# Reordering GpSimd's scatters, two statistics and two rank requests at the end of layer 0's attention

## The chip, the cores and the metric

The kernel runs on one core of a Trainium2 chip, as one launch. The metric is device time in microseconds (us); lower is better. The time before is the median of three runs. The profile comes from one further execution of the same kernel, taken with the hardware profiler. Engine names are those of the profile: PE (TensorE, matrix products), DVE (VectorE), ACT (ScalarE), POOL (GpSimd), SP (SyncE, which here only issues DMAs).

## What is computed

The reference is two pre-norm transformer layers on x of shape (8, 1024, 128). This case lies in layer 0 alone, at the end of its attention and the start of its expert feed-forward:

```python
x = x + attention(layernorm(x))        # layer 0: 8 heads of 32, softmax over 1024 keys
n = layernorm(x)
logits = n @ gate_w.T                  # 14 experts
top2_p, top2_i = top_k(softmax(logits), 2)
w = top2_p / max(sum(top2_p), 1e-10)
x = x + (n + w0 * expert(top2_i[0], n) + w1 * expert(top2_i[1], n))
...                                    # layer 1: linear attention, then top-1 experts
```

`expert` is gelu(n @ w1 + b1) @ w2 + b2 with the weights of the chosen expert.

## The kernel before, in words

**Stage one, attention and routing.** For each of 8 batches the kernel makes softmax attention over 1024 tokens, eight heads as two groups of four. A *block* is a batch, a group and a half of the queries (512): 32 blocks in all. Each block takes 16 *steps* (8 key chunks `kc`, two steps `hp` each), so there are 512 steps, numbered h = 0 to 511. A list `todo[h]` holds pieces of other work (the projections and routing of a batch that is done, the normalisation of a batch to come), put there by `at(h, f)`; the loop runs them at the end of step h. On PE, DVE and ACT the program order of the trace is the order of the queue. On POOL it is not: the tile framework's scheduler orders POOL, and the kernel holds single instructions back with `keep_in_program_order` (used through `pinned`), which adds an edge to the instruction traced just before on the same engine. Such an edge orders the issue only; it is no semaphore wait.

**The steps around the change.** From step 488 on the loop is "quiet": no more block's maxima are made, and the DVE takes over the sums of exponentials (L777) that POOL made until then. In a quiet pair of steps, PE makes four heads' scores, ACT makes their exponentials (L383), PE weighs values (`num`, L397) and, every other pair, sums columns for the denominators (`den`, L397). Steps 496 to 511 are those of the last block. Order of issue, before, in the steps that matter (chunk pairs of step h and h+1 share one tile of exponentials):

| step | of the attention | pieces from `todo` |
|---|---|---|
| 490 | scores, num | `rank` of batch 6: PE `rk` (L567, L570), DVE picks (L576) |
| 491 | den; DVE sums L777 | `places` of batch 6: DVE L585 to L590, writes the row numbers `at` |
| 492, 493 | scores, num | shares of batch 6 (L527 to L537) |
| 494 | scores, num | `project` of the first half of batch 7: PE `op` (L448), DVE adds x (L453); `norm` |
| 495 | den; DVE sums L777 | `stats` (L266, L268), `power` (DVE `ve` L273, POOL `rs`) of that half |
| 496 | scores, num | `offset` (DVE `off`, L278), `scaled` (ACT `xn`, L291) |
| 497 | num; ACT copies the finished num to `nums` (L425) | `scaled` (ACT `xn`) |
| 498 | scores, first num of the last block | `turned`: PE `tp` (L299), ACT `xT` (L301) |
| 499 | den; ACT copies den to `dens` (L410); DVE sums L777 | `logits` of the half (L471 to L477) |
| 499 to 502 | eight quotients: DVE reciprocal L415, POOL product | `first` to `third` |
| 504, 505 | scores, num | `count` (DVE L545 to L561), `rank` |
| 506, 507 | scores, num; den; DVE sums L777 | `places`, `softmax` |

PSUM has one bank for `num` and one for `den` (pool `pvd`), three for `st` (pool `sc`) and three for `big` (pool `big`, which also serves `rk`, `op`, `tp` and `lg`).

**Scatters.** `places` appends 16 closures per batch (two experts times eight chunks; eight for each half of batch 7) to `moving`. The loop pops one per step when quiet, before it runs `todo`. Each closure, `move` (L594), is an indirect DMA issued by POOL that writes 128 rows of `xn` into `rows_in` at the rows in `at`. All scatters stand in a group `rows_in` whose members are declared free of dependencies on each other (L599, L600), and then are kept in program order (L601). Batch 6's 16 scatters are traced at steps 494 to 509. Batch 7's first half has two at steps 510 and 511 and six after the loop; its second half's eight follow those.

**After the loop** the second half of batch 7 goes through one chain: reciprocals and quotients (DVE, L807, L808), `project`, `stats`, `power`, `offset`, `scaled`, `turned`, `choice`, then all scatters left.

**Stage two, experts.** Tiles of 256 rows are read back from `rows_in` by SP (L916); the first weights are copied by DVE (L924) behind the last scatter.

**GpSimd's line.** The power (`ALU.pow`), the quotients and the sums run under the helper's line, L209; they are told apart by their tiles (`rs`, `outT`, `e`).

Of the kernel before, what the change touches and what calls it, by code (L numbers as in the profile page):

```python
# [12 lines left out]
ALU = mybir.AluOpType  # L13
# [4 lines left out]
NB = 8  # L18
# [60 lines left out]
def tile_two_layers(  # L79
# [5 lines left out]
    nc = tc.nc  # L85
# [22 lines left out]
    mhalf = keep.tile([P, CPB], F32, name="mhalf")  # L108
# [6 lines left out]
    rstds = [keep.tile([P, CPB], F32, name=f"rs{b}", tag=f"rs{b}") for b in range(NB)]  # L115
# [45 lines left out]
    def looked_up(table, nt, engine, top):  # L161
# [12 lines left out]

        return value


    layer0 = ctx.enter_context(ExitStack())
    routes = layer0.enter_context(tc.tile_pool(name="routes", bufs=1))
# [10 lines left out]
    nc.gpsimd.memset(counts, 0.0)  # L190
    found = routes.tile([P, NB, 2, CPB], U32, name="found")
    last_move = []
    layer0w = ctx.enter_context(ExitStack())
    blob = layer0w.enter_context(tc.tile_pool(name="blob", bufs=1)).tile([P, E0, B_END], F32, name="blob")

    with ExitStack() as ph:
# [11 lines left out]
        def pinned(f, *args, **kw):  # L208
            return tc.keep_in_program_order(f(*args, **kw))  # L209
# [46 lines left out]
        class Norm:  # L256
# [13 lines left out]
            def power(self):  # L270
                cs = slice(self.c0, self.c0 + self.n)
                ve = stat0.tile([P, self.n], F32, name=f"ve{self.n}")
                nc.vector.tensor_scalar(ve, mvs[self.b][:, cs, 1], LN_EPS, None, ALU.add)  # L273
                pinned(nc.gpsimd.tensor_tensor, rstds[self.b][:, cs], ve, mhalf[:, :self.n], ALU.pow)

            def offset(self):
                cs = slice(self.c0, self.c0 + self.n)
# [125 lines left out]
        def settle(n, qb, pieces):  # L403

            b, g = divmod(n, 2)
            if (b, 0) not in outs:
                outs[b, 0] = work.tile([P, 2, T], F32, name="outT", bufs=1)
            out_b, top = outs[b, 0], tops.pop(0)
            s = work.tile([P, BLK], F32, name="dens", bufs=1)
            nc.scalar.copy(s, vds.pop((n, qb, True)))  # L410
            w = BLK // pieces

            def divide(i):
                cols = slice(i * w, (i + 1) * w)
                nc.vector.reciprocal(s[:, cols], s[:, cols])  # L415
                pinned(
                    nc.gpsimd.tensor_tensor,
                    out_b[:, g, qb * BLK + i * w:qb * BLK + (i + 1) * w], top[:, cols], s[:, cols], ALU.mult,
                )

            return [lambda i=i: divide(i) for i in range(pieces)]

# [11 lines left out]
        class Finish:  # L434
# [144 lines left out]
            def places(self):  # L579

                n, b, c0 = self.n, self.b, self.c0
                ats = [stat0.tile([P, CPB], U32, name=f"at{k}") for k in range(2)]
                for k in range(2):
                    mine = ranks[:, k, b, c0:c0 + n]
                    nc.vector.tensor_reduce(mine, self.picks[k], AX.X, ALU.add)  # L585
                    to = self.tile("to", [P, n])
                    nc.vector.scalar_tensor_tensor(
                        to, chosen[:, k, b, c0:c0 + n], float(UNIT * REG0), mine, ALU.mult, ALU.add
                    )
                    nc.vector.tensor_scalar(ats[k][:, :n], to, float(TW0), None, ALU.add)  # L590
                xn = self.xn

                def move(j, k):
                    ins = nc.gpsimd.indirect_dma_start(  # L594
                        out=rows_in, out_offset=bass.IndirectOffsetOnAxis(ap=ats[k][:, j:j + 1], axis=0),
                        in_=xn[:, c0 + j, :], in_offset=None,
                    )

                    tc.declare_no_dep(ins.ins, group="rows_in", reason="rows are distinct")  # L599
                    tc.add_to_no_dep_group("rows_in", ins.ins)  # L600
                    tc.keep_in_program_order(ins)  # L601
                    last_move[:] = [ins.ins.name]

                moving.extend(lambda j=j, k=k: move(j, k) for k in range(2) for j in range(n))
# [39 lines left out]
        norm = Norm(1, 0, CPB, xn, xT[1])  # L644
# [30 lines left out]
        def at(h, f, *args):  # L675
            todo[h].append(lambda: f(*args))

        def normalised(h0, norm, stats, power, offset, scaled, turned):
            for i, h in enumerate(stats):
                at(h0 + h, lambda i=i: norm[0].stats(2 * i))  # L680
            at(h0 + power, lambda: norm[0].power())
            at(h0 + offset, lambda: norm[0].offset())
            for i, h in enumerate(scaled):
                at(h0 + h, lambda i=i: norm[0].scaled(2 * i))
            for i, h in enumerate(turned):
                at(h0 + h, lambda i=i: norm[0].turned(CPK * i))
# [24 lines left out]
        def complete(b):  # L711

            h0, f, norm = 64 * (b + 1), Finish(b, 0, CPB), []
            at(h0 + 8, f.project, 0)
            at(h0 + 17, f.project, CPK)
            at(h0 + 10, lambda: norm.append(f.norm()))
            normalised(h0, norm, (12, 14, 20, 22), 22, 26, (27, 28, 29, 30), (29, 32))
            hs = (36, 38, 37, 42, 46, 50, 47, 54, 56, 58, 62, 66)
            if b == NB - 2:
                hs = (33, 34, 34, 38, 39, 40, 40, 41, 42, 43, 44, 45)  # L720
            for h, piece in zip(hs, f.choice()):
                at(h0 + h, piece)

        def last_half():

            h0, f, norm = 64 * (NB - 1), Finish(NB - 1, 0, CPK), []
            at(h0 + 46, f.project, 0)
            at(h0 + 46, lambda: norm.append(f.norm()))
            normalised(h0, norm, (47, 47), 47, 48, (48, 49), (50,))
            for h, piece in zip((51, 52, 53, 53, 54, 55, 55, 56, 57, 58, 59, 60), f.choice()):  # L730
                at(h0 + h, piece)

        for b in range(NB):
            if b:
                complete(b - 1)
            if b + 1 < NB:
                prepare(b + 1)
        last_half()


        weighing, summing, dividing = None, None, []
        h = 0
        for n, qb in blocks:
            for kc in range(CPB):
                for hp in range(2):
# [9 lines left out]
                    if kc % 2 == 0:  # L755
                        if weighing is not None:
                            weigh(*weighing, den=False, half=hp)
                            if hp == 1 and weighing[2] == CPB - 1:
                                numerator(*weighing[:2])
                    elif hp == 0:  # L760
                        weigh(*weighing, den=False)
                    elif summing is not None and h < STEPS - 1:
                        weigh(*summing, den=True)
                        if summing[2] == CPB - 1:
                            dividing = settle(*summing[:2], pieces=8)
                            dividing.pop(0)()
# [33 lines left out]
        f = Finish(NB - 1, CPK, CPK)  # L800
        norm = f.norm()
# [43 lines left out]
    nil1 = wts1.tile([P, TI0, RW1], F32, name="nil1")  # L845
    counts1 = keep.tile([P, E1], F32, name="counts1")
    rows1 = dram.tile([ROWS1, RW1], F32, name="rows1")

    def behind(ins, name, kind=mybir.DependencyClass.NoSync):
        tc.add_manual_dep(  # L850
            ins, name, mybir.DependencyInfo(kind, mybir.DependencyReason.DATA), reason="the order of issue"
        )

    def load_layer1():
        nc.sync.dma_start(out=wq1_sb, in_=wq1)
# [41 lines left out]
    def tiles0(ph, first, last):  # L897
# [23 lines left out]
        def stage(j):  # L921
            e = expert_of(j)
            t = work.tile([P, 1, B_END], F32, name="wt", bufs=4)
            ins = nc.vector.tensor_copy(t, blob[:, bass.ds(e, 1), :]).ins  # L924
            if j == 0:

                behind(ins, last_move[0], mybir.DependencyClass.Sync)
            return t[:, 0, :]
# [114 lines left out]
    with ExitStack() as ph:  # L1043
# [22 lines left out]
        def stats(p):  # L1066

            x1 = tokens_of(p)
            st = stat1.tile([P, PAIR, 6], F32, name="bnst1")
            mv = stat1.tile([P, PAIR, 2], F32, name="mv1", bufs=6)  # L1070
            for i in range(PAIR):
                nc.vector.bn_stats(st[:, i, :], x1[:, i, :])
                nc.vector.bn_aggr(mv[:, i, :], st[:, i, :])
            ve = stat1.tile([P, PAIR], F32, name="ve1")
            nc.vector.tensor_scalar(ve, mv[:, :, 1], LN_EPS, None, ALU.add)
            rs = stat1.tile([P, PAIR], F32, name="rs1", bufs=6)
            ins = tc.keep_in_program_order(nc.gpsimd.tensor_tensor(rs, ve, mhalf[:, :PAIR], ALU.pow)).ins
            if gathered[0] == PAIR * NPAIR:
                for name in since:
                    behind(ins, name)  # L1080
            since.clear()
            norms[p] = mv, rs
# [22 lines left out]
        def behind_within(ins):  # L1105

            if products:
                behind(ins, products.pop(), mybir.DependencyClass.Sync)
# [782 lines left out]
```

## Time and profile before

| what | value |
|---|---|
| median of three runs (lowest, highest) | 2073.74 us (2072.45, 2079.61) |
| the profiled execution, its own time | 2022.9 us |
| span in its profile, first to last instruction | 2021.0 us |
| mean granted TensorE clock | 0.959 of full speed |
| busy share PE, DVE, ACT, POOL | 95%, 68%, 55%, 59% |
| scatters L594, all | 128, mean 1018 ns |
| scatters L594, issue to landing (median, 1215 to 1320 us) | 2.3 us |

The profile's page gives busy time by engine, the busy share in 40 slices of the span, and the costliest groups of instructions. Three further views are used below. The timeline of an engine lists its instructions in order of time: start, duration, engine, line and operation, written tile <- read tiles, count; in brackets the idle time of the engine just before, and what ended it. The table of windows gives for each stretch of time the busy time of each engine, and the granted TensorE clock as a fraction of full speed. The view of waits sums who waited for whom. All times count from the span's start. Attention fills the span up to about 1280 us; the experts' first matrix products follow at 1313 us.

### The profile page before, as it was taken

The page shows a single profiled execution, that of the slowest core. Times are in us where ns is not written, and L with a number is a line of the kernel's source. Part 1 is how long each engine was busy: PE and PEld are TensorE (multiplying, and loading weights), DVE is VectorE, ACT ScalarE, POOL GpSimd, SP SyncE. Part 2 cuts the span into 40 slices and gives each one's busy share as a digit, 9 for nine tenths or more (in the row PEclk, how much of TensorE's full clock was granted, in tenths as well). Part 3 has the DMA queues.
Part 4 walks back from the last instruction along what each step waited for, and adds up shares of the span by engine and source line. Part 5 has one row for each costly group of instructions (what it writes and reads, how often), then busy time and mean ns, then how long its engine had stood idle before and what let it go on. Part 6 is the DMA issues. An engine that isn't in the chain of part 4 may idle for free. (4 is left out here: it accounts for less than half of the span.)

```text
span 2021.0 us, 45115 instructions
## 1 busy us (share of the span) xinstructions
PE 1918.9 (95%) x17340; PEld 991.8 (49%) x17340; DVE 1379.7 (68%) x3551; ACT 1108.8 (55%) x2338; POOL 1201.7 (59%) x1312
## 2 busy tenths in 40 slices
PE   7999999999999999999999998499869999996997
PEld 3333333333333333333333333299847777775996
DVE  6677767768768768768767876566647777774453
ACT  3555565565565565565565455266546666662443
POOL 1466656667667667766766766433265576644455
PEclk9999999999999999999999998699969999996999
DMA  7000000000000000000000000044322221111332
GB/s 243 2 2 2 1 2 3 8 8 10 8 8 9 9 8 8 9 8 9 8 8 8 13 9 23 31 131 133 117 76 74 83 62 49 49 39 64 106 103 59
DMA packets 49407, 80.93 MB, mean 40 GB/s; under 512 B 13225, under 2 KB 32112, under 8 KB 49056
## 3 DMA queue, kind: packets, MB, share of 16 engines
q0 software_dynamic: 17552, 41.03, 6.2%
q1 hardware_dynamic: 28240, 28.97, 5.0%
q10 hardware_dynamic: 3392, 7.95, 1.3%
q8 instruction: 140, 2.29, 0.5%
q14 instruction: 83, 0.68, 0.1%
HBM read 42.08 MB, written 35.96 MB: 39 GB/s over the span
## 5 line engine op out<-in xcount | busy, mean ns | idle before, releaser
L344 DVE TENSOR_REDUCE nmp<-big 128x1 f32<-128x512 f32 x1000 | 642.1, 683 | 279.4 <-PE st L380 237.4
L383 ACT ACTIVATE e<-st 128x512 f32<-128x512 f32 x1000 | 544.1, 595 | 477.4 <-PE st L380 413.4
L209 POOL TENSOR_TENSOR e<-e 128x512 f32<-128x512 f32 x488 | 604.0, 1268 | 53.4 <-PE num L397 53.3
L340 PE MATMUL big<-kT,qT 32*128 32x512 f32 x2000 | 625.8, 640 | 0.7 <-DVE nmp L344 0.5
L380 PE MATMUL st<-qT,kT 32*128 32x512 f32 x2000 | 531.1, 588 | 0.0
L397 PE MATMUL num<-e,v 128*32 128x512 f32 x3064 | 301.4, 466 | 8.5 <-ACT nums L425 8.5
L209 POOL TENSOR_TENSOR outT<-nums,dens 128x64 f32<-128x64 f32 x248 | 80.7, 326 | 347.2 <-DVE dens L415 259.6
L380 PEld LDWEIGHTS st<-qT,kT 32*128 32x128 f32 x2000 | 213.9, 191 | 3.7 <-issue 1.7
L379 PE MATMUL st<-nb,ones_h 3*128 3x512 bf16 x1000 | 211.9, 384 | 0.0
L397 PEld LDWEIGHTS num<-e,v 128*32 128x32 f32 x3064 | 61.2, 108 | 296.2 <-issue 269.2
L379 PEld LDWEIGHTS <-ones_h 3*128 3x128 bf16 x1024 | 50.9, 91 | 310.2 <-issue 303.3
L340 PEld LDWEIGHTS big<-kT,qT 32*128 32x128 f32 x2000 | 191.9, 183 | 22.1 <-DVE nmp L344 18.3
L1116 POOL DMA_INDIRECT got<-rows_out,found x128 | 126.2, 986 | 97.0 <-PE tp L1151 46.6
L594 POOL DMA_INDIRECT rows_in<-xn,at x128 | 130.4, 1018 | 38.3 <-issue 29.4
L415 DVE RECIPROCAL dens<-dens 128x64 f32<-128x64 f32 x248 | 130.2, 537 | 17.5 <-ACT dens L410 17.4
L397 PE MATMUL den<-e,ones 128*32 128x512 f32 x1032 | 140.3, 610 | 0.2 <-POOL e L209 0.2
L1661 POOL DMA_INDIRECT out_x<-y,to x72 | 79.0, 1097 | 68.5 <-DVE y L1659 51.8
L1642 ACT ACTIVATE g<-ph,wt 128x256 f32<-128x256 f32 x144 | 63.8, 474 | 87.0 <-PE ph L1639 87.0
L964 POOL DMA_DIRECT2D rows_out<-y x68 | 39.6, 582 | 95.1 <-DVE y L961 87.9
L1171 ACT ACTIVATE qm<-qk,cst 128x256 f32<-128x256 f32 x128 | 54.6, 497 | 53.1 <-DVE qk L1168 53.1
L1421 POOL DMA_INDIRECT rows<-row,where x64 | 63.9, 999 | 29.1 <-issue 13.0
L952 PEld LDWEIGHTS py<-wt,g 128*128 128x128 f32 x576 | 76.2, 193 | 3.8
(289 smaller groups left out, 2916.6 us busy)
## 6 DMA issues: line engine op xcount, KB each, us to landing
xr<-rows SPq DMA_DIRECT2D x36, 257.0 KB
xr<-rows_in SPq DMA_DIRECT2D x72, 128.0 KB
rows_out<-y POOLq DMA_DIRECT2D x68, 128.0 KB, 2.3
nb<-part SPq DMA_DIRECT2D x384, 1.0 KB
blob<-in_blob ACTq DMA_DIRECT2D x8, 578.0 KB
blob<-in_blob SPq DMA_DIRECT2D x1, 4494.0 KB
x<-in_x SPq DMA_DIRECT2D x8, 512.0 KB
rows<-nil ACTq DMA_DIRECT2D x9, 257.0 KB
```

The costliest lines, as they stand in the source:

```text
L209: return tc.keep_in_program_order(f(*args, **kw))
L340: nc.tensor.matmul(ps, lhsT=qTs[n][r, qc * P:(qc + 1) * P], rhs=kTs[n][r, kb * BLK:(kb + 1) * BLK], start=True, stop=True,)
L344: nc.vector.tensor_reduce(nmps[n][:, h, qc, kb:kb + 1], ps, AX.X, ALU.max, negate=True)
L379: nc.tensor.matmul(st, lhsT=ones_h[r3, :], rhs=nbs[n][r3, cols], start=True, stop=False)
L380: nc.tensor.matmul(st, lhsT=kTs[n][r, kc * P:(kc + 1) * P], rhs=qTs[n][r, cols], start=False, stop=True)
L383: nc.scalar.activation(e[:, h, :], st, AF.Exp, scale=SCALE0)
L397: nc.tensor.matmul(vds[key][32 * h:32 * h + 32, cols], lhsT=ones[:, :HD0] if den else vs[b][:, kc, c0:c0 + HD0], rhs=e[:, h, cols], start= ...
L415: nc.vector.reciprocal(s[:, cols], s[:, cols])
L594: ins = nc.gpsimd.indirect_dma_start(out=rows_in, out_offset=bass.IndirectOffsetOnAxis(ap=ats[k][:, j:j + 1], axis=0), in_=xn[:, c0 + j, : ...
L952: nc.tensor.matmul(ps[:, i, :], lhsT=g[:, k, i * P:(i + 1) * P], rhs=w[:, B_W2 + k * D:B_W2 + (k + 1) * D], start=k == 0, stop=k == K0 - 1,)
L1116: ins = tc.keep_in_program_order(nc.gpsimd.indirect_dma_start(out=gots[p][:, i, k, :], out_offset=None, in_=rows_out, in_offset=bass.Indir ...
L1661: ins = nc.gpsimd.indirect_dma_start(out=out_rows, out_offset=bass.IndirectOffsetOnAxis(ap=at[:, i:i + 1], axis=0), in_=y[:, i, :], in_off ...
```

## The change

Four edits:

1. A list `last_own` holds the name of the last power or quotient that was traced for POOL. Every scatter of batches 6 and 7 gets one more edge, behind that instruction. It orders the issue only. (`behind` is moved up in the file; it is the same function.)
2. For the first half of batch 7, `stats` and `power` are asked for at step 494, right behind `project` and `norm`, instead of at step 495. In the DVE's queue they so stand ahead of the sums (L777) of step 495.
3. Batch 6: `rank` at step 491 instead of 490, `places` at 492 instead of 491.
4. First half of batch 7: `rank` at step 506 instead of 505, `places` at 507 instead of 506, `softmax` at 508 instead of 507.

No instruction is added or removed, and no tile, buffer or transfer changes.

```diff
+    def behind(ins, name, kind=mybir.DependencyClass.NoSync):
+        tc.add_manual_dep(
+            ins, name, mybir.DependencyInfo(kind, mybir.DependencyReason.DATA), reason="the order of issue"
+        )
...
+    last_own = []
...
             def power(self):
...
-                pinned(nc.gpsimd.tensor_tensor, rstds[self.b][:, cs], ve, mhalf[:, :self.n], ALU.pow)
+                ins = pinned(nc.gpsimd.tensor_tensor, rstds[self.b][:, cs], ve, mhalf[:, :self.n], ALU.pow)
+                last_own[:] = [ins.ins.name]
...
             def divide(i):
...
-                pinned(
+                ins = pinned(
                     nc.gpsimd.tensor_tensor,
                     out_b[:, g, qb * BLK + i * w:qb * BLK + (i + 1) * w], top[:, cols], s[:, cols], ALU.mult,
                 )
+                last_own[:] = [ins.ins.name]
...
                     tc.keep_in_program_order(ins)
+                    if b >= NB - 2:
+                        behind(ins.ins, last_own[0])
                     last_move[:] = [ins.ins.name]
...
             if b == NB - 2:
-                hs = (33, 34, 34, 38, 39, 40, 40, 41, 42, 43, 44, 45)
+                hs = (33, 34, 34, 38, 39, 40, 40, 41, 43, 44, 44, 45)
...
-            normalised(h0, norm, (47, 47), 47, 48, (48, 49), (50,))
-            for h, piece in zip((51, 52, 53, 53, 54, 55, 55, 56, 57, 58, 59, 60), f.choice()):
+            normalised(h0, norm, (46, 46), 46, 48, (48, 49), (50,))
+            for h, piece in zip((51, 52, 53, 53, 54, 55, 55, 56, 58, 59, 60, 60), f.choice()):
                 at(h0 + h, piece)
```

Here `h0` is 448 in both places, and `choice()` lists, in order: logits, first, exponentials, second, third, fourth, exponential2, count, rank, places, softmax, weights.

More of the change, by code (lines that the diff above doesn't have):

```diff
@@ L847, in tile_two_layers @@
     rows1 = dram.tile([ROWS1, RW1], F32, name="rows1")
[L849 to L852, printed above, removed]
     def load_layer1():
```

## The prediction

> **What bounds the kernel now.** I read the page first, then the windows, the waits, and the timeline of each engine from 1220 to 1310 us. The page's 40 slices are 50.5 us each:
>
> ```profile
> PE   7999999999999999999999998499869999996997
> PEclk9999999999999999999999998699969999996999
> ```
>
> PE is full except where stages meet. Slices 25 and 26 (from 1212 us) have two holes: the end of the last block, and the serial chain behind it. The change acts on the first. The timelines follow it back, PE, ACT, DVE, POOL:
>
> ```profile
> 1228.04 0.47 PE L567 MATMUL rk<-both,cst 128*128 128x112 f32 x2 [1.20 <-DVE both L554]
> ...
> 1249.64 1.94 PE L397 MATMUL num<-e,v 128*32 128x512 f32 x8 [8.48 <-ACT nums L425]
> ...
> 1266.54 0.43 PE L567 MATMUL rk<-both,cst 128*128 128x56 f32 x2 [1.71 <-DVE both L554]
> ```
> ```profile
> 1248.24 0.88 ACT L291 ACTIVATE xn<-x,off,rs 128x128 f32<-128x128 f32 x2 [7.38 <-DVE off L278]
> 1249.03 0.56 ACT L425 COPY nums<-num 128x512 f32<-128x512 f32 x1
> ```
> ```profile
> 1237.23 2.49 DVE L777 TENSOR_TENSOR e<-e 128x512 f32<-128x512 f32 x4
> ...
> 1240.96 0.17 DVE L273 TENSOR_SCALAR ve<-mv 128x4 f32<-128x4 f32 x1
> 1248.05 0.16 DVE L278 SCALAR_TENSOR_TENSOR off<-mv,rs 128x4 f32<-128x4 f32 x1 [6.91 <-POOL rs L209]
> ```
> ```profile
> 1233.33 0.96 POOL L594 DMA_INDIRECT rows_in<-xn,at  x1 [0.78 <-DVE ranks L585]
> ...
> 1245.99 0.96 POOL L594 DMA_INDIRECT rows_in<-xn,at  x1 [0.30 <-issue]
> 1246.96 1.05 POOL L209 TENSOR_TENSOR rs<-ve,mhalf 128x4 f32<-128x4 f32 x1
> ...
> 1276.97 0.96 POOL L594 DMA_INDIRECT rows_in<-xn,at  x1 [0.30 <-issue]
> 1288.06 1.04 POOL L209 TENSOR_TENSOR rs<-ve,mhalf 128x4 f32<-128x4 f32 x1 [10.12 <-DVE ve L273]
> 1289.30 1.03 POOL L594 DMA_INDIRECT rows_in<-xn,at  x1 [0.20 <-issue]
> ...
> 1299.70 0.96 POOL L594 DMA_INDIRECT rows_in<-xn,at  x1 [9.37 <-issue]
> ```
>
> Read upwards: eleven scatters of batch 6 run in a row, 1.27 us apart; the power `rs`, whose input `ve` is there at 1241.13, starts at 1246.96; `off` waits for it, ACT's `xn` for `off`, and the copy `nums` stands behind `xn` in ACT's queue. The single `num` bank is free only then: PE stands 8.48 us. The clock pays too:
>
> ```profile
> 1244.39:1249.64 5.25, 0.00 (x0) 0.00 (x1) 0.16 (x1) 1.40 (x4) 4.03 (x5) 0.50 0.11 37
> 1249.64:1254.64 5.00, 5.00 (x21) 1.35 (x22) 0.00 (x0) 3.26 (x8) 0.00 (x0) 0.50 0.04 13
> 1264.87:1268.28 3.41, 1.71 (x16) 1.04 (x16) 2.77 (x13) 1.10 (x3) 1.02 (x1) 1.00 0.06 20
> 1268.28:1271.69 3.41, 3.41 (x20) 0.59 (x16) 1.50 (x6) 2.06 (x4) 2.27 (x3) 0.50 0.09 31
> ```
>
> The third number from the end is the granted clock: half for 5.00 us of work behind the long wait, and for 3.41 us behind the wait of 1.71.
>
> **Does the new edge bind?** Batch 6 has 16 scatters, traced at steps 494 to 509. Those traced right behind an own POOL instruction (496 behind the power, 499 to 502 behind quotients) are five, and the timeline has five at their places (1248.21, then between the quotients). The other eleven stand behind a scatter of their own group, and eleven ran early. So the pin between neighbours of the group seems to be lost, and the edge to the last power or quotient restores it. Before the power only step 494's scatter then remains.
>
> **The sum, step by step.**
>
> *Rank of batch 6.* PE no longer waits 1.20 for `both`: the `den` products (about 1.1, the last quarter held to about 1228.0 by POOL's sum, which ends at 1227.50) fill the gap, and scores of step 492 start at about 1229.0, not 1229.90. But the DVE now picks behind the sums: 1228.65 + 2.85 + 0.4 = 1231.9. Until then `rk` holds a `big` bank that the scores of step 494 want, which began at 1232.11 and needed their second bank at 1232.38. PE keeps 0.4 of the 0.9. Row numbers `at` come no later, as `places` stood behind the sums already.
>
> *Statistics and power.* `op` ends at 1236.2; x 0.69, statistics 1.3, `ve` 0.2: 1238.4 (before 1241.13). POOL has one scatter, at about 1233, so `rs` runs 1238.5 to 1239.6. What is late next is the DVE: the sums of step 495 (2.49) now stand between `ve` and `off`, so `off` ends at 1241.0, not at 1239.8. ACT's exponentials end at 1240.5; `xn` at 1241.05, `nums` 1241.84 to 1242.4, `num` at 1242.45: 7.2 us before 1249.64. PE still stands about 1.65 us.
>
> *Clock.* With no long hole, `num`, `tp` and `den` run in 2.6 us instead of 4.77 (1249.64 to 1254.41). Part of this is lost again: `xT` comes only when ACT is done with the exponentials of step 498. `dens` goes 1254.63 to 1245.6, and the DVE, busy without a break from 1255.25 on, starts 9.1 us earlier. PE hangs on it at 1259.5 (a `big` bank, 0.29 behind `pr`), so 9.1 is the gain there.
>
> *Rank of batch 7's half.* In the old frame: scores of step 506 at 1264.83 (two banks free, the others when ACT is done at 1264.5 and 1265.0), `num` at 1266.1, `rk` at 1267.1 (`ahead` is there at 1266.94), `den` 1267.95, scores of 508 at 1268.95 instead of 1272.06. That is 3.1: the wait of 1.71 and 1.4 of half clock. Cover: picks, sums and `places` then fill the DVE until about 1274.5; its next work at the end begins at 1276.6. `den` of step 509 needs sums that end at 1271.0 and comes at 1271.15: just covered; each us that the DVE loses there is lost.
>
> Here the trace and the Trainium skill differ ("TensorE: Matmul & The Clock Gate", Part 1 and its table of goals): idle gaps up to about 3 us are said to leave the clock up, half speed coming after an idle window of about 3.4 us. The drops at 1206.84, 1244.39 and 1268.28 are 11 and 7 windows of 3.41 apart, so the window is as stated. But the last follows a window in which PE was busy 1.71 of 3.41. By the rule this rank is worth 1.7, by the row 3.1; I take the row. The same row speaks against the new gap of 1.65: a window with some 57% busy lies between 50% (gated) and the 79% at 1227.32 to 1230.73 (2.69 of 3.41, not gated). Price: nothing to 1.7, most of it absorbed by PE's waits for `xT` and `pr`; I take 0.5.
>
> *Scatters moved.* Four (steps 495 to 498) queue behind `rs`, until 1244.9; the first quotient comes at about 1246.8. Seven (503 to 509) leave for behind the last quotient (1264.46, now 1255.4), with 502, 510 and 511: 10 x 1.27, to 1268.1; the second power is due at 1275.9. The last six of the first half, five of which ran early, go behind that power: 6 x 1.27 = 7.6, 1277.1 to 1284.7, and the last eight start at 1287.5 (1299.70 less 12.2). Slack 7.8 and 2.8; cost nothing. Their transfers land in 2.3 us, before those that SP's fetches wait for. `at` has two buffers; the next `places` of that buffer is near 1287, long after. A rule speaks against this ("SBUF — State Buffer", section on the bandwidth-pool intuition): a DMA issued by GpSimd of some 620 ns takes 3100 beside a DVE copy, since its descriptors wait. The nearest row is the scatter at 1289.30, which stood beside a scaling, a memset and a copy on DVE: 1.03 against 0.96. By the row the cost is zero, by the rule 18.7 (below).
>
> *Sum.* 9.1 + 3.1 - 0.5 = 11.7. Profiled execution: 2022.9 - 11.7 = 2011.2. The median of the runs, 2073.74, is 50.8 longer; no view shows where, so I carry the microseconds over (in proportion it were 12.0): 2062.0.
>
> **Rivals.**
> *Clock stays low* (0.22): the new gap or another phase of the window gates PE again, and the second rank brings only its wait: 7.2 + 1.7 = 8.9, 2064.8. For: half-busy windows were gated. Against: PE's next waits hide it.
> *The change doesn't do what it says* (0.11): scatters still run ahead, or `rs` waits for something else. Edits 3 and 4 alone bring 3.1: 2070.6. Against: the count of eleven.
> *Scatters become the wait* (0.09): at price c each, ten before the second power are late by 10c - 20.5, six behind it by 6c - 10.4. From c = 2.05 and 1.73 they cost; 16c - 30.9 eats 12.2 at c = 2.69; at 3.1 it is 18.7, so 6.5 slower: 2080.2. For: the rule. Against: no scatter in the window took over 1.50.
>
> **How the numbers follow.** The likeliest case has 0.58, its own range 2060 to 2064. 0.5% is 10.4 us, about what a measurement of this kernel can tell from no change: faster means below 2063.4. Of the first case 0.52 lies there, of the clock's 0.03: 0.55. Slower means over 2084.1, c over 3.34: 0.04. Same: 0.41. The range leaves out the last rival and half of the second: 2058.5 to 2070.0.
>
> **What would show it.** `rs` after one scatter of batch 6, near 1238.5; the wait for `nums` under 2 us; clock near full from 1244 to 1272; no wait for `both` before either in-loop `rk`; the last eight scatters still released by `ranks` or issue at their usual distance (10.6 us) from `rs`. I am wrong if `off` still waits for `rs`, if PE waits at the `big` bank of step 494 longer than it saved, or if the scatters behind the second power push the last eight.

## The result, and the profile after

The changed kernel takes 2055.12 us (median of 6 runs, 2047.79 to 2059.5), the kernel before on the same chip 2072.81 (6 runs, 2064.37 to 2079.61): ratio 0.9932, 95% interval 0.9910 to 0.9954, which is 14.1 us of 2072.8. (The quotient of the two medians is 0.9915, or 17.7 us, inside that interval; the text keeps to the ratio.) On another chip, where everything is quicker (before 2057.34, 36 runs), it took 2043.9 (22 runs): 0.9944, interval 0.9923 to 0.9965, 11.5 us. The prediction was 11.7 us, inside both intervals. Its range of 2058.5 to 2070.0 us stood on a time before of 2073.74: at the ratio 0.9932 that is 2059.6, in the range; the median measured, 2055.12, is below it.

The chain that the prediction followed, in the profile after (span 2053.8, its run 2055.6); first PE, then ACT, DVE and POOL:

```profile
1227.76 0.47 PE L576 MATMUL rk<-both,cst 128*128 128x112 f32 x2
...
1241.62 1.07 PE L405 MATMUL num<-e,v 128*32 128x512 f32 x8 [1.81 <-ACT nums L434]
...
1259.85 0.43 PE L576 MATMUL rk<-both,cst 128*128 128x56 f32 x2
```
```profile
1240.22 0.88 ACT L299 ACTIVATE xn<-x,off,rs 128x128 f32<-128x128 f32 x2 [0.71 <-DVE off L286]
1241.00 0.56 ACT L434 COPY nums<-num 128x512 f32<-128x512 f32 x1
```
```profile
1237.51 0.17 DVE L280 TENSOR_SCALAR ve<-mv 128x4 f32<-128x4 f32 x1
1237.59 2.52 DVE L788 TENSOR_TENSOR e<-e 128x512 f32<-128x512 f32 x4
1240.03 0.15 DVE L286 SCALAR_TENSOR_TENSOR off<-mv,rs 128x4 f32<-128x4 f32 x1
```
```profile
1233.49 0.95 POOL L603 DMA_INDIRECT rows_in<-xn,at  x1 [0.30 <-issue]
1237.77 1.42 POOL L216 TENSOR_TENSOR rs<-ve,mhalf 128x4 f32<-128x4 f32 x1 [3.32 <-DVE ve L280]
1239.39 1.03 POOL L603 DMA_INDIRECT rows_in<-xn,at  x1 [0.20 <-issue]
...
1280.98 1.04 POOL L216 TENSOR_TENSOR rs<-ve,mhalf 128x4 f32<-128x4 f32 x1 [9.47 <-DVE ve L280]
...
1292.62 0.96 POOL L603 DMA_INDIRECT rows_in<-xn,at  x1 [4.30 <-issue]
```

Both waits of PE for `both` are gone, and the wait for `nums` fell from 8.48 to 1.81 us. The power now waits for its input, not for scatters; between `ve` and `off` stand the four sums of step 495, as foreseen. The second power is reached at 1280.98 (before: 1288.06).

Two things are not as foreseen. The first is the clock (third number from the end, windows of the same profile):

```profile
1239.40:1242.81 3.41, 1.60 (x14) 0.35 (x11) 0.78 (x3) 2.70 (x8) 2.80 (x3) 1.00 0.12 41
1242.81:1246.22 3.41, 3.41 (x16) 1.42 (x16) 0.01 (x1) 2.53 (x6) 1.10 (x2) 0.50 0.11 38
1246.22:1253.05 6.83, 6.83 (x45) 2.95 (x45) 6.69 (x19) 2.20 (x5) 4.34 (x8) 0.50 0.03 10
1253.05:1259.88 6.83, 6.83 (x69) 2.11 (x65) 4.90 (x15) 5.40 (x12) 5.56 (x8) 1.00 0.13 42
```

It is half for 10.24 us behind the wait of 1.81. The second stands at steps 505 to 507; PE, then DVE and ACT:

```profile
1262.64 1.05 PE L405 MATMUL num<-e,v 128*32 128x256 f32 x10
1264.25 0.67 PE L405 MATMUL num<-e,v 128*32 128x256 f32 x4 [0.56 <-issue]
1265.68 0.38 PE L405 MATMUL num<-e,v 128*32 128x256 f32 x1 [0.76 <-issue]
```
```profile
1264.28 0.22 DVE L585 TENSOR_TENSOR cand<-rk,oh__13262 128x56 f32<-128x56 f32 x1 [5.55 <-remote]
```
```profile
1265.79 0.60 ACT L391 ACTIVATE e<-st 128x512 f32<-128x512 f32 x1 [5.02 <-remote]
```

In brackets, `remote` stands where the profile finds no instruction that ended the wait, `issue` where it shows nothing that was waited for. Sixteen products `num` take from 1262.64 to beyond 1266, where two pairs of steps earlier (1256.42) they took 1.07 us. DVE and ACT wait for signals of PE's work that was done long before: `rk` ended at about 1260.5, and `cand` starts at 1264.28. Meanwhile POOL issues scatters in a row, the last at 1263.44. I call this a late episode.

A slip of count, before the rest: `places` is the tenth piece of the choice, so batch 5's last scatter goes at step 492 and those of batch 6 are traced at steps 493 to 508, not 494 to 509, and those of batch 7's first half at 509 to 511 and behind the loop. So two scatters stand before the first power, not one, and five behind the second (four of them moved). The counts of eleven and of what is moved stay, and nothing in the sum hung on it.

### The profile page after: what moved, and what is told of

It reads as the page before. It is cut to its first block, busy times and chain, and to the rows that moved or that the text cites. A ratio compares the mean times of both kernels' runs of the same rounds, so it can differ in the third digit from the quotient of the medians.

```text
span 2053.8 us, 45114 instructions
## 1 busy us (share of the span) xinstructions
PE 1941.6 (95%) x17340; PEld 1002.5 (49%) x17340; DVE 1376.3 (67%) x3551; ACT 1107.8 (54%) x2338; POOL 1201.0 (58%) x1312
## 3 DMA queue, kind: packets, MB, share of 16 engines
q8 instruction: 140, 2.29, 0.5%
## 5 line engine op out<-in xcount | busy, mean ns | idle before, releaser
L1122 POOL DMA_INDIRECT got<-rows_out,found x128 | 126.3, 987 | 93.7 <-PE tp L1157 36.5
L603 POOL DMA_INDIRECT rows_in<-xn,at x128 | 129.8, 1014 | 33.6 <-issue 24.9
L1667 POOL DMA_INDIRECT out_x<-y,to x72 | 78.9, 1096 | 68.2 <-DVE y L1665 51.2
L1083 POOL TENSOR_TENSOR rs<-ve,mhalf 128x2 f32<-128x2 f32 x64 | 46.3, 724 | 90.8 <-DVE ve L1081 65.9
```

Source lines behind the costliest of these rows:

```text
L603: ins = nc.gpsimd.indirect_dma_start(out=rows_in, out_offset=bass.IndirectOffsetOnAxis(ap=ats[k][:, j:j + 1], axis=0), in_=xn[:, c0 + j, : ...
L1122: ins = tc.keep_in_program_order(nc.gpsimd.indirect_dma_start(out=gots[p][:, i, k, :], out_offset=None, in_=rows_out, in_offset=bass.Indir ...
L1667: ins = nc.gpsimd.indirect_dma_start(out=out_rows, out_offset=bass.IndirectOffsetOnAxis(ap=at[:, i:i + 1], axis=0), in_=y[:, i, :], in_off ...
```

## The experiments

Profiled executions are compared by the stage, since the rest of the span has a spread of its own. Times in the table are us from the start of POOL's last sum of exponentials (`e<-e`, 1222.44 in the first profile of before, 1219.3 to 1222.4 in all), from which on the kernels differ. "x add" is where DVE adds `op`, "power" the first power, "dens" ACT's copy of the denominators. "Second power" is the end of the local chain; the copy `wt`, with which the next stage begins, comes 22.7 to 23.0 behind it in all runs but e7 (27.6). A ratio stands where several runs were made, otherwise the time of the one run.

| run | time, or ratio | x add | power | PE's wait for `nums` | `dens` | second power |
|---|---|---|---|---|---|---|
| before, first | 2022.9 | 14.2 | 24.5 | 8.48 | 32.2 | 65.6 |
| e1 before | 2067.24 | 26.6 | 31.2 | 3.73 | 38.1 | 74.3 |
| e8 before | 2069.83 | 26.8 | 31.4 | 2.39 | 39.1 | 77.0 |
| after, first | 0.9932 | 13.8 | 16.1 | 1.81 | 23.9 | 59.3 |
| e2 after | 2061.36 | 13.8 | 16.1 | 1.78 | 23.3 | 57.4 |
| e12 after | 0.9944 | 13.7 | 16.0 | 1.72 | 22.9 | 59.6 |
| e3 scatters only | 2065.89 | 17.0 | 21.6 | 2.72 | 27.3 | 66.5 |
| e4 all but scatters | 2076.80 | 20.8 | 24.5 | none | 35.7 | 72.9 |
| e5 `nums` first | 0.9942 | 13.8 | 16.1 | 0.23 | 22.0 | 57.7 |
| e6 paced | 0.9921 | 13.8 | 16.1 | 1.82 | 23.4 | 57.0 |
| e7 late twelve | 2058.25 | 13.8 | 16.1 | 1.82 | 23.5 | 53.8 |
| e9 gap | 0.9917 | 13.7 | 16.0 | 1.72 | 24.2 | 54.5 |
| e10 gap, `nums` first | 0.9911 | 13.7 | 16.0 | 0.23 | 21.9 | 51.8 |
| e11 idle sums | 2058.04 | 13.7 | 24.7 | 9.26 | 32.4 | 68.2 |

Runs e1 to e4 shared a chip (before there: 2073.99, one run), e5 to e8 another (2070.36, 12 runs), e9 to e12 a third (2057.34, 36 runs). Intervals: e5 0.9911 to 0.9973, e6 0.9892 to 0.9950, e9 0.9888 to 0.9946, e10 0.9887 to 0.9935.

**Both kernels once more (e1, e2, later e8 and e12), no edit.**

> The kernel before once more, to see which part of its first profile (2021.0 us) is typical. Stage measured: from the start of GpSimd's last sum of exponentials to the start of its last power (65.6 us in the first profile, 59.3 after the change). If the long wait is the order of the scatters, the stage is 65 to 66 again, eleven scatters run before the first power and PE waits 8 to 9 us for nums. If the part behind layer 0 (708 us from the experts' first product to the end in the first profile, 747 after the change) is noise that the change has no part in, it is near 745 here; if the change lengthened it, it is near 708.

> The changed kernel once more. Its first profile has two losses in the last block: half clock for 9.6 us behind a PE wait of 1.81 us, and about 3 us in which PE's signals came late to DVE and ACT (near 1264 us). If the second is an accident of one execution, the stage (last sum to last power) is 56 to 57 us here; if it belongs to the order of the instructions, 59 again. The clock: if gating follows the phase of the window, the half-speed stretch is shorter or absent in this run, and the stage 54 to 57.

The first profile of before was the odd one. In e1 the eleven scatters make a late episode too; POOL, PE, DVE and ACT of e1:

```profile
1231.23 0.96 POOL L594 DMA_INDIRECT rows_in<-xn,at  x1 [0.78 <-DVE ranks L585]
...
1243.86 0.96 POOL L594 DMA_INDIRECT rows_in<-xn,at  x1 [0.31 <-issue]
1251.58 1.04 POOL L209 TENSOR_TENSOR rs<-ve,mhalf 128x4 f32<-128x4 f32 x1 [6.76 <-DVE ve L273]
```
```profile
1241.46 5.16 PE L397 MATMUL num<-e,v 128*32 128x256 f32 x10
1246.97 1.12 PE L397 MATMUL num<-e,v 128*32 128x256 f32 x6 [0.35 <-issue]
```
```profile
1246.99 0.69 DVE L453 TENSOR_TENSOR x<-op,x 128x512 f32<-128x512 f32 x1 [13.73 <-remote]
```
```profile
1247.11 0.60 ACT L383 ACTIVATE e<-st 128x512 f32<-128x512 f32 x1 [10.95 <-remote]
```

The product `op` had ended at 1236.1; `x` is added at 1246.99, some 3 us behind the issue of the last scatter. The power then waits for `ve`, not for POOL: the stall that the prediction removed is not there in this form, and a longer one stands ahead of it. e2 repeats the changed kernel (57.4), with the late episode at the same place (ACT waits 5.06 us for a remote signal).

The first profile hid one more cost, that of batch 6's rank. PE waits 1.20 us for `both` in all three profiles of before. In the first no half clock follows; in e1 it does for 3.41 us, in e8 for 6.83. The product `op` ends 14.1 us behind the start of POOL's sum in the first profile, 15.7 in e1, 17.1 in e8, and 13.6 in every profile with edit 3, where neither the wait nor this half clock is there.

> The kernel before, a third time. Theory A (the eleven scatters in a row delay PE's signals in most executions, and the first profile was an exception): the product num runs over 4 us long under the row, x add waits over 10 us, the stage takes 70 to 75 us. Theory B (that was the second profile's exception): x add comes about 14 us behind POOL's last sum, the stage takes 64 to 67 us.

It is theory A: x add 26.8 us behind the sum, second power at 77.0, though by the expectation's band (70 to 75) it is even later. The product that is slow is another one (`num` took its 1.93 us at 1247.60, at half clock; a `den` before it and the scores of 1240.3 to 1247.6 were late).

> The changed kernel again, on the chip of these three runs, for comparison: ratio near 0.993, the stage 57 to 60 us, x add at 13.8 us, the power at 16.1 us, late signals at steps 506 to 508 that cost some 3 to 5 us.

As expected, but for the episode at steps 506 to 508, which cost over 5 us: from the exponentials of 1257.80 to the next at 1266.92 is 9.1, where e9, below, takes 3.2 for that pair.

**One part alone (e3, e4).** e3 has the scatters' order alone, e4 the other three edits without it:

```diff
 e3: -            normalised(h0, norm, (46, 46), 46, 48, (48, 49), (50,))
     +            normalised(h0, norm, (47, 47), 47, 48, (48, 49), (50,))
     (and the two lists of steps as in the kernel before)
 e4: -                    if b >= NB - 2:
     -                        behind(ins.ins, last_own[0])
```

> Edit 1 alone: scatters behind the last power or quotient; statistics and ranks as before. By my theory the power starts right when its input is there (about 0.1 us behind ve), PE's wait for nums falls from 8.5 to 2.5 to 3 us, and both waits of PE for the sums of the two ranks (1.2 and 1.7 us) stay: stage 58 to 60 us. By the rival (the statistics and ranks bring the gain) the stage stays above 63.

> Edits 2, 3 and 4 without edit 1: statistics ahead, ranks later, scatters free as before. By my theory eleven scatters run before the first power, PE's wait for nums stays at 8 to 10 us, and only the ranks' waits go: stage 62 to 64 us. By the rival that the order of the scatters is not what held the power the wait is gone and the stage is 56 to 59.

Both missed their bands. In e3 the power starts 0.09 us behind `ve` and PE's wait for `nums` is 2.72, as expected, but the stage is 66.5, not 58 to 60. PE of e3 shows the first loss:

```profile
1225.92 0.59 PE L576 MATMUL rk<-both,cst 128*128 128x112 f32 x2 [1.21 <-DVE both L563]
...
1227.08 1.94 PE L405 MATMUL den<-e,ones 128*32 128x512 f32 x8
```

`den` takes 1.94 us at half clock (1.07 at full), which lasts 6.83 us, and `op` ends at 17.0, not at 13.6. The rest is lost between `dens` and the second power (39.2 us; 35.4 in the mean of the changed kernel): the wait for the second rank (1.78), half clock behind it, and a late episode (ACT waits 7.08 us for a remote signal). In e4 eleven scatters run before the power again, as expected, but PE does not wait for `nums`: it comes later than `nums` itself, with gaps of 0.80 to 0.96 us in its products from 17.9 to 25.0, for which the profile shows no cause, and the stage is 72.9, not 62 to 64.

Means of three profiles each: second power at 72.3 before, at 58.8 after. e3's 66.5 and e4's 72.9 both lie within the 65.6 to 77.0 of the kernel before, so one profile each does not divide these 13.5 among the edits. What they show is where losses lie: the first rank's wait and half clock are there without edit 3 (e3) and gone with it (e4), and the eleven scatters run ahead, and make PE late, without edit 1 (e4).

**The rest of the wait for `nums` (e5).**

```diff
-            normalised(h0, norm, (46, 46), 46, 48, (48, 49), (50,))
-            for h, piece in zip((51, 52, 53, 53,
+            normalised(h0, norm, (46, 46), 46, 48, (49, 49), (51,))
+            for h, piece in zip((52, 52, 53, 53,
```

> The changed kernel, with the scaling xn of batch 6 asked for one step later, so that ACT's copy nums no longer stands behind it in the last block. Theory A (the remaining wait of 1.81 us and the half clock behind it cost what the first sum did not count): PE's wait for nums falls below 0.7 us, no half clock comes right behind it, and the stage from POOL's last sum of exponentials to the second power takes 54 to 58 us, against 57.4 and 59.3 in the two profiles of the changed kernel; time 1 to 3 us below it. Theory B (xT and pr hide it): the wait goes too, but turned comes later, PE waits there instead, stage 57 to 60 us, time within 1 us of the changed kernel.

The wait falls to 0.23, no half clock follows, and `dens` comes 1.4 us earlier (22.0, after 23.4 in the mean). At the second power nothing of it is left: a late episode at step 507 takes it (ACT waits 6.82 us for a remote signal).

**What makes the episode (e6, e7).** e6 lets each scatter from step 503 on wait for the last exponential traced before it. e7 takes none from the queue after step 504, so twelve stand behind the second power:

```diff
 e6: +                        if pace[0]:
     +                            behind(ins.ins, last_exp[0], mybir.DependencyClass.Sync)
     (pace[0] = h >= 503 in the loop; last_exp is set where ACT's exponential is issued)
 e7: -                    if moving and (quiet or h % 4 == 2):
     +                    if moving and (quiet or h % 4 == 2) and h < 505:
```

> The changed kernel, with each of the scatters of batch 6 from step 503 on also waiting for the last exponential traced before it, so that the six in a row before the second power are spread over their steps. Theory A (a row of indirect scatters makes signals to and from PE late until its last one has landed): the late arrivals at the third rank (cand 5.55 us from a remote wait, ACT 5.02) are gone or under 3 us, the stage takes 53 to 56.5 us against 57.4 and 59.3, and the time is 2 to 4 us lower. Theory B (chance, or work that comes at that place anyway, such as instruction fetch): the late arrivals stay, stage 57 to 60, time the same within 1 us.

> The changed kernel, with the scatters of batch 6 not taken from their queue after step 504, so that more of them (12 in place of 5 of that batch's last and its neighbours) stand between the second power and the last eight. The row of twelve should take 12 x 1.27 = 15.2 us against a slack of some 10.6: the last scatter comes about 25.4 us behind the second power, where every run so far had 20.5. Theory A (rows hurt PE only where PE signals): the six before the second power are gone, so the stage before it is shorter (54 to 57 us), and all but that is given back at the end: time 0 to 3 us above the changed kernel. Theory B (scatters cost nothing while PE is at the tail, the tail has more slack than the gap shows): last scatter 20.5 to 22 us behind the power, time 1 to 4 us lower.

Pacing failed: exponentials come so often that the gaps grew to 1.3 to 2.0 us only, and the episode came at step 507 (ACT waits 3.20 for a remote signal). The stage of e6, 57.0, is in theory B's band. Leaving the scatters out of that stretch, in e7, ends it: second power at 53.8, just below theory A's band. The price is where it was expected: the last scatter comes 25.3 us behind the power, against 20.5, and the stage's end is where it was (`wt` at 81.4; after: 80.1 to 82.4).

**A version without it (e9, e10).** No scatter at steps 505 to 509; four at the end, which wait for the last exponential; eight in place of five behind the second power:

```diff
-                        moving.pop(0)()
+                        for _ in range(0 if 505 <= h < 510 else 2 if h >= 510 else 1):
+                            moving.pop(0)()
 (with e6's wait from step 505 on; e10 adds the edit of e5)
```

> The changed kernel, with no scatter of batch 6 between steps 505 and 509: its last four wait for the last exponential of the block, and the batch's eight others of the half stand behind the second power (8 in place of 5). Theory A (scatters issued while PE still has scores and products to do make its signals late; behind the second power there is room for 8 x 1.27 = 10.2 us before the last eight, which start 11.6 us behind it): no remote waits above 3 us at steps 506 to 509, the stage from POOL's last sum to the second power takes 53.5 to 55 us against 57.4 and 59.3, the last scatter stays 20.5 us behind the power, and the time is 3 to 5 us below the changed kernel's. Theory B (the lost time at that place comes with anything that POOL or the queues do late): the wait moves to the four late scatters, stage 56.5 us or more, time within 1.5 us of the changed kernel.

> The run before this one, and the scaling of batch 6 asked for a step later, so that ACT's copy nums is not behind it. If the gain of that copy (dens 1.3 us earlier, no half clock behind it) was only hidden by the late signals at steps 506 to 508, it shows now: stage 52 to 54 us, 1 to 1.5 below the run before. If it is taken back by the later xT and pr, the stage stays within 0.5 us of it.

PE and POOL of e9 at the same place:

```profile
1259.74 1.07 PE L406 MATMUL num<-e,v 128*32 128x256 f32 x16
...
1262.93 1.06 PE L406 MATMUL num<-e,v 128*32 128x512 f32 x8
```
```profile
1257.22 0.96 POOL L604 DMA_INDIRECT rows_in<-xn,at  x1 [0.30 <-issue]
1265.34 0.96 POOL L604 DMA_INDIRECT rows_in<-xn,at  x1 [7.16 <-ACT e L392]
...
1274.65 1.04 POOL L217 TENSOR_TENSOR rs<-ve,mhalf 128x4 f32<-128x4 f32 x1 [4.55 <-DVE ve L281]
```

The products run at 1.07 for sixteen with no gap. The last scatter is 20.7 us behind the power, so eight fit there. Second power at 54.5, within the expected band; with `nums` first at 51.8, even a little below it. So e5's gain was real and had only been eaten. Both beat the kernel before, at 0.9917 and 0.9911 of its time. Against the changed kernel on the same chip (0.9944) the intervals overlap: by time alone the 5.6 and 6.8 us are likely, not settled; by the stage, one profile each against the mean of three (58.8), they are 4.3 and 6.9 us.

**The stall rebuilt without scatters (e11).** In front of the first power of the changed kernel, behind the two scatters there, POOL gets a memset and nine sums on a tile of its own:

```diff
+                    idle = nc.gpsimd.memset(tile, 0.0)
+                    behind(idle.ins, last_move[0])
+                    for _ in range(9):
+                        last, idle = idle, nc.gpsimd.tensor_tensor(tile, tile, tile, ALU.add)
+                        behind(idle.ins, last.ins.name)
 (and the power is ordered behind the last of them)
```

> The changed kernel, with a memset and nine sums of 128x512 on a tile that nobody reads put on POOL in front of the first power, as long as the nine scatters that the change took from there (work is added, none left out). The power then starts about 24 to 25.5 us behind POOL's last sum of exponentials, where the kernel before had it at 24.5. Theory A (what those scatters cost is of two kinds: POOL's time, which every execution pays, and late signals of PE under them, which most executions pay): x add stays at 13.8 us, PE waits 7 to 9 us for nums, and the stage takes 62 to 66 us, as in the first profile of the kernel before (65.6), not 72 to 77 as in its other two. Theory B (the second part comes from POOL being busy, or from where the power stands, not from the scatters): x add comes at over 20 us, stage 70 us or more.

POOL, DVE and PE of e11:

```profile
1233.15 11.36 POOL L287 TENSOR_TENSOR idle<-idle 128x512 f32<-128x512 f32 x9
1244.47 1.04 POOL L216 TENSOR_TENSOR rs<-ve,mhalf 128x4 f32<-128x4 f32 x1
```
```profile
1233.43 0.69 DVE L472 TENSOR_TENSOR x<-op,x 128x512 f32<-128x512 f32 x1 [1.30 <-PE op L467]
```
```profile
1247.14 1.93 PE L415 MATMUL num<-e,v 128*32 128x512 f32 x8 [9.26 <-ACT nums L444]
```

With POOL as busy, but by sums, `x` is added at once and PE's wait for `nums` is the first profile's (9.26; 8.48 there), `dens` too (32.4; 32.2). So in this profile a busy POOL did not make signals late. It is one profile, and the first of before had no late signals under scatters either; what ties them to scatters is the count over all fourteen. `x` is added over 20 us behind POOL's sum in three of the four profiles with eleven scatters ahead of it (e1, e4, e8), and in none of the ten others. Behind a row of six or more in the last block ACT waits 3.2 to 7.1 us for a remote signal in all seven other profiles that have one (after, e2, e3, e5, e6, e11, e12), and in none of the three without (e7, e9, e10). The second power, 68.2, lies between the two theories' bands: this kernel kept the row of scatters at steps 503 to 508, and ACT waited 6.68 us there.

## Why the prediction was right, and where it was not

*What bounds, and the new edge:* right. Scatters no longer stand between `ve` and the power, in every profile of the changed kernel.

*Statistics and power:* right. The power came at 1237.77 (foreseen 1238.5), `off` ended at 1240.18 (1241.0), `num` at 1241.62 behind a wait of 1.81 (1.65). Counted from POOL's sum, whose start differs by 0.78 between the profiles, these are as foreseen within 0.2 us. `dens` was foreseen 23.2 behind that sum and came 22.9 to 23.9.

*Rank of batch 6:* right that its wait would go, too low in the price. The sum kept 0.4 for it; `op` ends 0.6 us earlier than in the first profile, but 2.2 to 3.6 earlier than in e1, e3 and e8, where half clock followed the same wait. That the first profile had none of it was luck of that execution.

*The term of 9.1* is that time less `dens` of before (1254.63 less 1245.6 is 9.0), and there the size failed. Against the first profile it is 32.2 - 23.4 = 8.8. Against the mean of the three profiles of before (36.5) it is 13.1. The profile that the prediction was made from did not show the late episode under the eleven scatters nor the half clock behind the first rank, which both others have. That this execution was an exception stood in its numbers (2022.9, where the three timed runs took over 2072), and the prediction only carried the difference over as "no view shows where". Part of it was in this very stage: e1 and e8 reach its end 6.6 and 9.1 us later. Most of it (38 of 44 to 47 us) lies behind the stage, which takes 710 us in that profile, and 733 to 760 us in all thirteen others, whichever kernel.

*The term of 3.1 (second rank).* Its wait is gone and the scores follow at full clock, but from `dens` to the second power the changed kernel took 35.4 us in the mean, not less than the first profile's 33.4. In e9, where no scatter stands at steps 505 to 509, it took 30.3: 3.2 less than the first profile. By that profile the term was sized rightly and was eaten. Against the mean of the three profiles of before (35.9), 0.5 remains.

*The step that failed* is "Slack 7.8 and 2.8; cost nothing". It asked what scatters do to POOL's queue and to the transfers behind them, and there it holds: in the stage and behind it all but three or four of 34 in each profile took 0.95 to 1.03 us, and none over 1.50; the last eight stayed 11.6 us behind the second power. The 3.1 us that the Trainium skill ("SBUF — State Buffer", section on the bandwidth-pool intuition) gives for a GpSimd DMA beside a DVE copy showed in no run; but no DVE copy beside a scatter took over 0.44 us, so no run here puts that rule to the test. But a row of scatters delays PE's signals and products, and PE was on the path. The rows' remains at steps 503 to 508 cost the changed kernel 4.3 us at the second power (58.8 less e9's 54.5). The two misses point in opposite ways: 13.1 + 0.5, together 13.5 before rounding, by the stage, where the sum had 9.1 + 3.1 - 0.5 = 11.7; by time 14.1 and 11.5. That the total came so close is in part luck: one term was some 4 us too small, the other some 2.6 too large.

*Clock.* "Near full from 1244 to 1272" was wrong in the first profile after: half for 10.24 us. The same wait of 1.72 to 1.82 us was followed at once by half clock for 10.24 and 3.41 us (after, e9) and by none in e2, e6, e7 and e12 (e2 has 3.41 us of it only 9 us later). Where it was followed, the wait lay in one window of 3.41 us, with PE busy 1.60 us of it in the first profile after and 1.75 in e9; in e2 and e12 it lay across the bound of two windows, with PE busy 2.29 to 2.82 in each. The cost is small, as the sum had it: `dens` at 22.9 to 23.5 without and at 23.9 and 24.2 with it, so the rival "clock stays low" was half true in its cause and wrong in its price of 2.8. The wait kept within the goal of no PE-idle gaps over about 3 us (the Trainium skill, "TensorE: Matmul & The Clock Gate", "Why this matters for your kernels"), and half clock came in two of six profiles all the same.

*The other rivals.* "Doesn't do what it says" is out: eleven scatters became two. "Scatters become the wait" failed by its mechanism, a price above 1.73 in POOL's queue.

*What stays open* is how scatters make PE late. PE's instruction packets are no cause that shows: they start at the same place of PE's order in all runs (its 19,875th recorded instruction, and within 20 of the 20,140th) and took 0.96 to 1.46 us, in and out of the episodes. Nor do the scatters' own packets differ: 95 and 97 ns in the mean, 10 to 25 us behind POOL's sum, in e1 and e8, 97 in the first profile of before. No run put plain transfers of POOL in the scatters' place, and all of this is read from profiled executions. How many scatters in what time it takes is open too: rows of four and three made none, rows of six to eleven in attention did, except in the first profile of before. Why that execution was spared is not known.

## What to carry to other kernels

Look at a second profile before a stall's price is taken from the first, above all where the profiled execution's time lies outside the timed runs. Ask of a row of indirect DMAs not only what it does to its own queue, but what PE does meanwhile; a test is to put plain work of the same length in its place. Scatters that nobody waits for are best put where PE waits anyway, here behind a power.

## What the runs showed of the hardware

- Under rows of six or more indirect scatters by POOL, 1.26 us apart, work on PE in attention came late by some 3 to 11 us, in every profile with such a row there but the first of before: sixteen products of 1.07 us took 3.6 (after, from 1262.64) and 6.6 us (e1, from 1241.46), and DVE and ACT waited for results that the records show as done (`op` in e1 ended at 1236.1, its reader started at 1246.99), and the way from `dens` to the second power took 33.6 (e6) to 36.7 us (e12), where e9 took 30.3. Behind the second power, where PE has little to do, rows of five and eight made no difference that shows: `wt` comes 22.7 to 23.0 us behind it in all runs but e7. The last late reader started 1.7 to 4.8 us behind the issue of the row's last scatter. Nine sums on POOL, 11.36 us in a row, did nothing of the kind in the one profile that had them (e11).
- The clock's half-speed stretches were multiples of 3.41 us in every profile, and the same wait was or was not followed by one from execution to execution: 1.20 us for the first rank in three of four profiles, 1.72 to 1.82 us for `nums` in two of six.
- The kernel before took 2073.99 us (one run), 2070.36 (median of 12) and 2057.34 (median of 36) on the three chips of the experiments: only ratios of one chip are compared here.
